# Decoder layer on one core: the first pair of the output projection in seven block products, with its weight sums and its loads in other places

## The chip, the cores and the metric

The kernel runs on one core of a Trainium2 chip. The metric is the device time of one execution in microseconds (us); the time of a kernel is the median of its runs. The engines are named PE (TensorE), DVE (VectorE), ACT (ScalarE), POOL (GpSimd) and SP (SyncE, which here only issues DMAs). Everything is float32.

## What is computed

One decoder layer over 2048 tokens (32 sequences of 64) of width 512: an attention with 32 heads of 128, a cross attention and a mixture of expert biases, each added to x. Only the attention's end matters here: every head's output is put beside the others to 4096 numbers per token, and the output projection `out @ Wo + bo` brings them back to 512.

```python
x = x + _L0_attn_ref(_layernorm(x), Wq, bq, Wk, bk, Wv, bv, Wo, bo, gq, gk)
#   ... per head: q, k, v; rmsnorm of q and k; softmax(q k^T * scale) @ v  -> out
#   return out @ Wo + bo          # (2048 x 4096) @ (4096 x 512)
x = x + _L0_xattn_ref(_layernorm(x), ctx_1024, ...)
x = x + _L0_ffn_ref(_layernorm(x), router_weight, router_bias, expert_bias)
```

## The kernel before

The 2048 tokens are 16 tiles of 128 rows. Two tiles (`t` = 2 pair, 2 pair + 1) are a pair, so there are 8 pairs; four tiles are a quad. The heads go in 16 groups of two. The main loop (L1259) runs over two halves of the tokens, and in each half over the 16 groups; a `Window` (L624) makes q, k and v of one group for the two quads of a half. The attention of a unit (one group, one quad; named 14_3 for group 14, quad 3) follows one window later, by a `Line` (L1153): `scale` multiplies k on POOL (L542) and q on DVE (L544) by the inverse roots `rs` that SP has fetched (L533), `attend` makes the scores on PE (L555), the softmax on DVE, ACT and POOL (L257 to L265), `turn` transposes the probabilities on PE (`pt_p`, L249), and the next `attend` mixes the values (L592), which ACT copies to `ot` (L607) and SP stores to HBM as `mixed` (L614).

When the last window is done, two units more have to be attended, 15_2 and 15_3, and 14_3 has to be finished. `drain` (L1358) does this, and fills PE's time between its steps with the output projection of pair 0. For that, three things are fetched: the mixtures of pair 0 (`a` with tile and head of the group: a0_0, a0_1, a1_0, a1_1; 1 MB each, L821), the weights Wo in four blocks B11, B12, B21, B22 of (head of the group, half of the columns), each in two parts of 1 MB (L809; `wo_0` holds B11 and B21, `wo010` and `wo011` are B12, `wo110` and `wo111` are B22), and the tiles x0, x1 of x.

Pair 0 is done plainly (`plain_out`, L850): for each of two tiles and two halves of the columns, two terms of 16 matmuls (`chunks`, L832, which yields every four matmuls, so that `drain` can count them), and an addition to x. Pairs 1 to 7 are done in Strassen-Winograd's form by `strassen_out` (L884): seven products of 16 matmuls instead of eight, numbered 1 to 7, with sums of mixtures (S) on the left and sums of weights (T) on the right. The weight sums are made once, by `wo_sums` (L864): two subtractions into `t1` and `t2` (L873, L874), one into `t4` (L878) for each half of the part index on DVE, and B22 - B12 (L881) on POOL. Each is an operation on 128 x 2048 numbers.

Pair 1's first products come next, and between them the small setup of the cross attention: `xw` and other weights are loaded, transposed (`pt_xw`, L1429), copied by ACT (`turned`), multiplied to `wqk`. From there `strassen_out` of pairs 1 to 7 yields every four matmuls, and `advance` (L1348) puts one step of the finished tiles' cross attention and experts (`after_attention`, L1105) in between.

What sets the order: PE, DVE, ACT and POOL follow the program's order up to `ordered.close()`; SP's queue is ordered by a scheduler, and so are DVE, ACT and POOL after that point. SP issues in order, and a DMA that has to wait for its buffer holds back those behind it. Buffers come from pools: `blocks` has seven of 1 MB, which hold the tokens' inputs of a half (x1 to x7) and later mixtures, weights and `t4`, and two of 4 MB, which hold the weights of the heads and later `wo_0` and `wo_t`; `xpool` has four of 256 KB for tiles of x and the bias (`bo_0`), so that x3 takes the place of `bo_0` when L825 has added the bias to x1.

The order in `drain` before, with `go(n)` for n steps of four matmuls:

```python
go(1); line.turn(); go(4); line.scale(); go(4); line.scale(); go(3); line.attend()
line.scale(); go(4); line.scale(); go(1); line.turn(); go(2); line.attend()
go(4); line.turn(); go(1); line.attend()
a12 = load_mixed(2, 1, block("a12_1"))
sums = wo_sums(wo_b)
next(sums)
for _ in fill: pass
```

Of the kernel before, what the change touches and what calls it, by code (L numbers as in the profile page):

```python
# [13 lines left out]
P = 128  # L14
# [27 lines left out]
def decoder_layer(  # L42
# [37 lines left out]
    def block(name):  # L80
        return blocks.tile([P, BLK], F32, tag="blk", name=name)
# [193 lines left out]
    class AttentionInput:  # L275
# [32 lines left out]
        def turn(self):  # L308
            pair = self.pair
            pt = [  # L310
                transposed(xt.rearrange("p (kc k) -> p kc k", k=P), f"a{2 * pair + i}", ps_s)
                for i, xt in enumerate(self.xs)
            ]
            half, t, j = pair // 4, pair // 2 % 2, pair % 2
            if pair % 4 == 0:


                halves_x[half] = {o: block(f"x{o}_{half}") for o in (1, 2, 4, 5, 6, 7, 3)}
            raw = {
                o: it[:, 0 : 8 * P].rearrange("p (c t j n) -> p c t j n", c=2, t=2, j=2)  # L320
                for o, it in halves_x[half].items()
            }
# [501 lines left out]
    def add_bias(xt):  # L824
        nc.gpsimd.tensor_tensor(xt, xt, bo_b, ALU.add)  # L825
# [21 lines left out]
    def out_block(name):  # L847
        return ps_a.tile([P, DH], F32, tag="pa", name=f"py_{name}")

    def plain_out(pair, a, b, done):  # L850
        ts = (2 * pair, 2 * pair + 1)
        xs = [load_x(t) for t in ts]
        for i, t in enumerate(ts):
            for n in range(2):
                py = out_block(f"{t}_{n}")
                yield from chunks(py, [(a[i][k], b[k][n]) for k in range(2)])
                to = xs[i][:, bass.ts(n, DH)]
                nc.vector.tensor_tensor(to, to, py, ALU.add)
                yield
        for t, xt in zip(ts, xs):  # L860
            add_bias(xt)
            done(t, xt)

    def wo_sums(b):  # L864

        four = four_blocks("wo_t")
        t1, t2 = (
            [it.rearrange("p (g f) -> p g f", f=DH) for it in two] for two in (four[0:2], four[2:4])
        )
        t4 = []  # L870
        for half in range(2):
            b11, b12, b21, b22 = (b[k][n][half] for k in range(2) for n in range(2))
            nc.vector.tensor_tensor(t1[half], b12, b11, ALU.subtract)  # L873
            nc.vector.tensor_tensor(t2[half], b22, t1[half], ALU.subtract)  # L874
            if half == 1:
                yield
            t4.append(block(f"wo_t4{half}").rearrange("p (g f) -> p g f", f=DH))
            nc.vector.tensor_tensor(t4[half], b21, t2[half], ALU.subtract)  # L878
        for half in range(2):
            b12, b22 = (b[k][1][half] for k in range(2))  # L880
            nc.gpsimd.tensor_tensor(b12, b22, b12, ALU.subtract)  # L881
        yield {1: b[0][0], 2: b[1][0], 3: b[1][1], 4: t4, 5: t1, 6: t2, 7: b[0][1]}

    def strassen_out(pair, right, done, a12=None):  # L884

# [373 lines left out]
    for n, (hg, half) in enumerate(groups):  # L1259
        w = weights.pop(n)  # L1260
        units = [HeadGroup(hg, 2 * half + t, w) for t in range(2)]
        prepare(n)
        if hg == 0:
            single(
                units[0],
                {
                    3: lambda: coming[0].norm(),
                    6: lambda: (coming.pop(0).turn(), coming[0].norm()),
                    11: lambda: coming.pop(0).turn(),
                },  # L1270
            )
# [25 lines left out]
        else:  # L1297
            more = {
                (0, 3): [lambda n=n: sums_of_next(n), lambda: make(1)],
                (1, 0): [lambda: make(1)],  # L1300
                (1, 3): [lambda: make(1)],
                (2, 3): [lambda: make(2)],
            }

            def also(n, m, it):
                more.setdefault((n, m), []).append(it)

            if hg == 1:
                for at, o in (
                    ((0, 0), 2),  # L1310
                    ((0, 1), 6),
                    ((0, 2), 3),
                    ((1, 0), 7),
                    ((1, 1), 3),
                    ((1, 2), 4),
                    ((2, 1), 4),
                ):
                    also(*at, lambda o=o: inner(o))
            if half == 0 and 2 <= hg < 2 + NT // 2:
                norm = normed_tile(NT // 2 + hg - 2)  # L1320
# [12 lines left out]
            if n + 1 == len(groups):  # L1333
                four = four_blocks("wo_0")
                wo_b = [[load_wo(k, 0, four[2 * k : 2 * k + 2])] for k in range(2)]
                a_0 = [[load_mixed(0, h, block(f"a0_{h}")) for h in range(HG)]]
            double(Window(units, w, half), more)
    for k in range(2):
        wo_b[k].append(load_wo(k, 1, [block(f"wo{k}1{i}") for i in range(2)]))


# [6 lines left out]
    def advance():  # L1348
        for it in list(tails):
            it[0] -= 1  # L1350
            if it[0] < 0:
# [3 lines left out]
                else:  # L1355
                    it[0] = wait

    def drain():  # L1358
        fill = iter(todo)

        def go(count):
            for _ in range(count):
                next(fill)
                take_waiting()

        go(1)
        line.turn()
        go(4)
        line.scale()
        go(4)  # L1370
        line.scale()
# [11 lines left out]
        go(1)  # L1383
        line.attend()
        a12 = load_mixed(2, 1, block("a12_1"))
        sums = wo_sums(wo_b)
        next(sums)
        for _ in fill:
            pass
        return a12, sums  # L1390

    rest = work.tile([P, BLK], F32, tag="qk", name="a1_1", bufs=4)
    bo_b = xpool.tile([P, D], F32, tag="x", name="bo_0")
    load(bo_b, bo.partition_broadcast(P))
    a_0.append([load_mixed(1, 0, block("a1_0")), load_mixed(1, 1, rest)])
    todo = plain_out(0, a_0, wo_b, start_tail)
    a12, sums = drain()
    assert not waiting and not coming
    ordered.close()
    phase.close()  # L1400
    work = ctx.enter_context(tc.tile_pool(name="output", bufs=2, reuse_waits="tile"))
    bo_b = work.tile([P, D], F32, tag="bo", name="bo_b", bufs=1)
    load(bo_b, bo.partition_broadcast(P))
    (right,) = sums
    outs = {1: strassen_out(1, right, start_tail, a12)}
    next(outs[1])

# [13 lines left out]
    nc.gpsimd.memset(eb_sb[NEXP:P, :], 0.0)  # L1421
    nc.gpsimd.memset(wds, 0.0)
    load(eb_sb[0:NEXP, :], eb)
    for _ in range(4):
        next(outs[1])

    pt = ps_t.tile([P, 2, P], F32, tag="pt", name="pt_xw")
    for j in range(2):
# [63 lines left out]
```

## Time and profile before

| | us |
|---|---|
| median of 3 runs | 1933.31 (1930.85 to 1934.56) |
| the profiled execution | 1932.7, its span 1930.9 |
| PE busy | 1887.6 (98%) |
| DVE, POOL, ACT busy | 1228.4, 1044.3, 646.8 |
| output projection on PE (L837): its two larger groups of matmul records | 262.5 (1152 records) and 144.3 (608 records) |

| stretch, us from the start | PE busy | DVE busy | granted PE clock | DMA share |
|---|---|---|---|---|
| 1350 to 1380, end of the last window | 29.78 of 30 | 20.26 | 1.00 | 0.95 |
| 1380 to 1400, pair 0 begins | 18.66 of 20 | 4.11 | 1.00 | 0.87 |
| 1400 to 1420 | 20.00 of 20 | 4.67 | 1.00 | 0.25 |
| 1420 to 1440 | 20.00 of 20 | 13.18 | 1.00 | 0.44 |
| 1440 to 1460, pair 1 begins | 14.57 of 20 | 15.06 | 0.94 | 0.31 |
| 1460 to 1480 | 18.29 of 20 | 6.46 | 0.89 | 0.39 |
| 1480 to 1500 | 20.00 of 20 | 10.22 | 0.91 | 0.19 |

In the lines of the timelines below, the columns are: start and length in us, engine, line, operation, output <- input by their names, shapes, and how many were merged; in brackets the idle time ahead of it and what ended it. A float32 matmul of PE leaves two records. Buffer numbers are left out of names, so `py` is any block of the projection, `wo_t` any of the weight sums.

### The profile page before, as it was taken

How to read it: one execution, taken by the hardware profiler on the slowest of the kernel's cores; microseconds unless marked ns; L12 is line 12 of the kernel's file. 1: busy time of each engine (PE TensorE's matmuls, PEld its weight loads, DVE VectorE, ACT ScalarE, POOL GpSimd, SP SyncE). 2: the span in 40 equal slices, each digit the busy share in tenths (PEclk: the TensorE clock that was granted, in tenths of full speed). 3: DMA queues.
4: the chain of work that ended last, by engine and by line, in shares of the span. 5: the costliest groups of instructions: out<-in, count | busy, mean ns of one | idle time of the engine just before them, and what ended most of it. 6: DMA issues, size and time to landing. Idle time of an engine off the chain costs nothing.

```text
span 1930.9 us, 40526 instructions
## 1 busy us (share of the span) xinstructions
PE 1887.6 (98%) x16877; PEld 1622.2 (84%) x16877; DVE 1228.4 (64%) x2024; ACT 646.8 (33%) x1579; POOL 1044.3 (54%) x812
## 2 busy tenths in 40 slices
PE   9999999999999999999999999999998999999997
PEld 8888888888888888888888888888886888888874
DVE  7867777676667659666666666666454545554554
ACT  2343344344333443344333434433311202221122
POOL 5856666665667539665666666565234323332320
PEclk9999999999999999999999999999998999999998
DMA  4244334334433343334433333444932231223100
GB/s 138 67 134 142 121 126 129 110 105 131 133 111 110 107 140 107 99 101 131 133 110 111 110 100 100 130 134 137 301 127 86 90 111 67 71 88 112 49 20 23
DMA packets 164568, 214.92 MB, mean 111 GB/s; under 512 B 10144, under 2 KB 135136, under 8 KB 160288
## 3 DMA queue, kind: packets, MB, share of 16 engines
q1 hardware_dynamic: 163200, 211.24, 34.1%
q8 instruction: 133, 2.18, 0.5%
q10 hardware_dynamic: 1184, 1.08, 0.2%
q14 instruction: 51, 0.42, 0.1%
HBM read 171.92 MB, written 40.37 MB: 110 GB/s over the span
## 4 chain that ended last, share of the span: by engine, by line
PE 76%; DVE 12%; POOL 7%; issue 3%; DMA 1%; ACT 1%; SPq 0%; POOLq 0%; DVEq 0%; ACTq 0%
PE p_w L655 24%; PE py L837 19%; PE va L387 7%; PE vb L387 6%; POOL qk L734 5%; PE ms_w L779 3%; PE s L555 3%; PE o L592 3%; DVE qk L666 3%; DVE qk L679 3%; DVE qk L544 1%; PE pt_p L249 1%; PE pa L445 1%; DVE sums L262 1%; PE py_x L1050 1%
## 5 line engine op out<-in xcount | busy, mean ns | idle before, releaser
L655 PE MATMUL p_w<-x,w 128*128 128x256 f32 x2940 | 723.9, 383 | 8.6 <-DVE qk L666 8.0
L655 PEld LDWEIGHTS p_w<-x,w 128*128 128x128 f32 x2940 | 521.2, 190 | 70.7 <-DVE qk L666 13.1
L666 DVE TENSOR_TENSOR qk<-p_w,qk 128x512 f32<-128x512 f32 x360 | 213.0, 600 | 135.0 <-PE p_w L655 99.1
L356 ACT ACTIVATE sq<-qk 128x512 f32<-128x512 f32 x256 | 158.1, 629 | 400.2 <-POOL qk L734 225.4
L387 PEld LDWEIGHTS va<-w,x 128*128 128x128 f32 x2048 | 263.6, 191 | 30.5 <-ACT v L403 20.6
L387 PE MATMUL va<-w,x 128*128 128x128 f32 x2048 | 276.1, 278 | 2.1 <-ACT v L403 2.1
L837 PE MATMUL py<-wo,a 128*128 128x256 f32 x1152 | 262.5, 381 | 0.0
L679 DVE TENSOR_TENSOR qk<-p_w,qk 128x512 f32<-128x512 f32 x360 | 220.1, 620 | 57.4 <-PE p_w L655 53.9
L120 POOL TENSOR_TENSOR w<-w 128x768 f32<-128x768 f32 x126 | 244.5, 1951 | 2.4
L837 PEld LDWEIGHTS py<-wo,a 128*128 128x128 f32 x1152 | 213.9, 190 | 35.6 <-issue 7.3
L265 POOL TENSOR_TENSOR prob<-prob,inv 128x512 f32<-128x512 f32 x64 | 75.3, 1177 | 294.9 <-DVE inv L264 291.7
L542 POOL TENSOR_TENSOR qk<-qk,rs 128x512 f32<-128x512 f32 x128 | 172.4, 1347 | 113.1 <-DMA rs<-row_w 92.9
L387 PEld LDWEIGHTS vb<-w,x 128*128 128x128 f32 x1536 | 201.4, 192 | 9.7
L387 PE MATMUL vb<-w,x 128*128 128x128 f32 x1536 | 202.4, 275 | 0.0
L403 ACT COPY v<-va 128x256 f32<-128x256 f32 x256 | 94.8, 370 | 308.9 <-PE va L387 308.7
L544 DVE SCALAR_TENSOR_TENSOR qk<-qk,gqk,rs 128x512 f32<-128x512 f32 x128 | 173.4, 1355 | 11.1 <-DMA rs<-row_w 10.0
L837 PE MATMUL py<-wo_t,a 128*128 128x256 f32 x608 | 144.3, 389 | 0.0
L837 PEld LDWEIGHTS py<-wo_t,a 128*128 128x128 f32 x608 | 116.1, 195 | 16.9 <-issue 0.8
L734 POOL TENSOR_TENSOR qk<-qk 128x512 f32<-128x512 f32 x60 | 90.7, 1511 | 61.1 <-DVE qk L679 58.7
L257 DVE TENSOR_REDUCE mx<-s 128x8 f32<-128x512 f32 x64 | 44.1, 689 | 106.8 <-PE s L555 106.8
L407 DVE TENSOR_TENSOR v<-vb,v 128x256 f32<-128x256 f32 x192 | 80.8, 421 | 45.6 <-PE vb L387 27.0
L607 ACT ACTIVATE ot<-o,bvt 128x256 f32<-128x256 f32 x256 | 99.2, 469 | 2.2 <-PE o L592 2.2
(182 smaller groups left out, 2198.2 us busy)
## 6 DMA issues: line engine op xcount, KB each, us to landing
rs<-row_w SPq DMA_DIRECT2D x120, 512.0 KB
mixed<-ot SPq DMA_DIRECT2D x64, 512.0 KB
a<-mixed SPq DMA_DIRECT2D x32, 1024.0 KB
w<-in_wq_dram SPq DMA_DIRECT2D x64, 256.0 KB
w<-in_wk_dram SPq DMA_DIRECT2D x62, 256.0 KB
w<-in_wv_dram SPq DMA_DIRECT2D x62, 256.0 KB
wo<-in_wo_dram SPq DMA_DIRECT2D x8, 1024.0 KB
x<-in_x_dram SPq DMA_DIRECT2D x20, 256.0 KB
```

The costliest lines, as they stand in the source:

```text
L120: on.tensor_tensor(*(it.rearrange("p c j d -> p (c j) d") for it in (out, a, b)), ALU.subtract)
L356: nc.scalar.activation(sq, of, AF.Square)
L387: nc.tensor.matmul(to[:, j, :], left[i][:, c, j, :], right[i][:, c, 2, :], start=first and j == 0 and c == 0, stop=c == 1, skip_group_chec ...
L403: nc.scalar.copy(self.v[h, ab], what)
L542: nc.gpsimd.tensor_tensor(k, k, rk, ALU.mult)
L544: lambda: nc.vector.scalar_tensor_tensor(q, q, gqk, rq, ALU.mult, ALU.mult)
L607: nc.scalar.activation(ot[:, h, :, b * SEQ : (b + 1) * SEQ], o[b][:, h, :, :], AF.Identity, bias=bvt[:, hg * HG + h : hg * HG + h + 1],)
L655: nc.tensor.matmul(bank[:, s, :], self.w.inner[o][i], inner_x[self.half, o][i], start=first and s == 0, stop=True, skip_group_check=True,)
L666: nc.vector.tensor_tensor(to(t, j), bank, add(t, j), ALU.add)
L679: nc.vector.tensor_tensor(to(t, j), bank, to(t, j), ALU.add)
L734: on.tensor_tensor(qk[to], qk[to], qk[what], ALU.add)
L837: nc.tensor.matmul(py, a[:, g, :], b[g // KH][:, g % KH, :], start=n == 0 and g == 0, stop=n == last and g == NHG - 1,)
```

## The change

- Pair 0 is done by `first_out`, in seven products in the order 1, 2, 3, 7, 5, 6, 4; the four sums of mixtures are made by DVE after the third to the sixth step of `drain`.
- The weight sums are made by DVE alone, one operation after each step from the ninth on.
- The mixtures of pair 0 are fetched inside the last window (a1_1 into a buffer of q and k, three into the `blocks`), ahead of the last weight blocks; B22 is fetched ahead of B12. The sum `s1` takes another buffer of q and k, `S4` a quarter of `wo_t`.
- `p1`, the first product, takes a buffer of `xpool`.
- The first `turn` in `drain` comes after two steps instead of one.
- Pair 1 goes six steps instead of four ahead of the setup of the cross attention, with `advance` called in the last two.
- The order in which the seven blocks x1 to x7 are asked for is another.

```diff
-                halves_x[half] = {o: block(f"x{o}_{half}") for o in (1, 2, 4, 5, 6, 7, 3)}
+                halves_x[half] = {o: block(f"x{o}_{half}") for o in (1, 2, 6, 5, 7, 3, 4)}
...
-    def plain_out(pair, a, b, done):
...
-    def wo_sums(b):
...
+    def wo_sums(b, places):
...
+        (b11, b12), (b21, b22) = b
+
+        def subtract(to, a, what):
+            nc.vector.tensor_tensor(to, a, what, ALU.subtract)
+
+        def make():
+            for half in range(2):
+                subtract(t1[half], b12[half], b11[half])
+                yield
+                subtract(b12[half], b22[half], b12[half])
+                yield
+            for half in range(2):
+                subtract(t2[half], b22[half], t1[half])
+                yield
+            for half in range(2):
+                t4.append(block(f"wo_t4{half}").rearrange("p (g f) -> p g f", f=DH))
+                subtract(t4[half], b21[half], t2[half])
+                yield
+
+        return {1: b11, 2: b21, 3: b22, 4: t4, 5: t1, 6: t2, 7: b12}, make()
+
+    def first_out(a, right, s4, s1, done):
+        (a11, a12), (a21, a22) = a
+        xa, xb = load_x(0), load_x(1)
+        la, ra, lb, rb_ = (xt[:, bass.ts(n, DH)] for xt in (xa, xb) for n in range(2))
+        p1 = xpool.tile([P, D], F32, tag="x", name="p1_0")[:, 0:DH]
+        def combine(op, to, x, y):
+            return lambda: nc.vector.tensor_tensor(to, x, y, op)
+
+        sums[3] = combine(ALU.add, s1, a21, a22)
+        sums[4] = combine(ALU.subtract, a21, a11, a21)
+        sums[5] = combine(ALU.subtract, a11, s1, a11)
+        sums[6] = combine(ALU.subtract, s4, a12, a11)
...
+        py = yield from product(1, a11)
+        nc.scalar.copy(p1, py)
+        nc.gpsimd.tensor_tensor(la, la, p1, ALU.add)
+        yield
+        py = yield from product(2, a12)
+        add(la, py)
+        yield
+        py = yield from product(3, s4)
+        add(ra, py)
+        yield
+        py = yield from product(7, a21)
+        add(lb, py)
+        add(rb_, py)
+        yield
+        py = yield from product(5, s1)
+        add(ra, py)
+        add(rb_, py)
+        yield
+        py = yield from product(6, a11)
+        add(p1, py)
+        for to in (ra, lb, rb_):
+            nc.gpsimd.tensor_tensor(to, to, p1, ALU.add)
+        add_bias(xa)
+        done(0, xa)
+        yield
+        py = yield from product(4, a22)
+        add(lb, py)
+        add_bias(xb)
+        done(1, xb)
...
-                a_0 = [[load_mixed(0, h, block(f"a0_{h}")) for h in range(HG)]]
...
+                also(2, 0, lambda: mixture(0, 1, lambda: block("a0_1")))
+                also(2, 1, lambda: mixture(1, 0, lambda: block("a1_0")))
+                also(2, 2, lambda: mixture(0, 0, lambda: block("a0_0")))
+                also(2, 2, lambda: mixture(1, 1, lambda: qk_buffer("a1_1")))
...
-    for k in range(2):
+    for k in (1, 0):
         wo_b[k].append(load_wo(k, 1, [block(f"wo{k}1{i}") for i in range(2)]))
...
             for _ in range(count):
-                next(fill)
+                next(todo, None)
+                done += 1
                 take_waiting()
-
-        go(1)
+                if done in sums:
+                    sums[done]()
+                elif done >= 9:
+                    next(making_wo, None)
+
+        go(2)
         line.turn()
-        go(4)
+        go(3)
         line.scale()
...
         line.attend()
         a12 = load_mixed(2, 1, block("a12_1"))
-        sums = wo_sums(wo_b)
-        next(sums)
-        for _ in fill:
-            pass
-        return a12, sums
...
+        go(4)
+        return a12
...
-    for _ in range(4):
+    for n in range(6):
         next(outs[1])
+        if n > 3:
+            advance()
```

More of the change, by code (lines that the diff above doesn't have):

```diff
@@ L848, in out_block @@
         return ps_a.tile([P, DH], F32, tag="pa", name=f"py_{name}")
-    def plain_out(pair, a, b, done):
[L851 to L862, printed above, removed]
@@ L864, in wo_sums @@
-    def wo_sums(b):
-        four = four_blocks("wo_t")
+    def wo_sums(b, places):
         t1, t2 = (
-            [it.rearrange("p (g f) -> p g f", f=DH) for it in two] for two in (four[0:2], four[2:4])
+            [it.rearrange("p (g f) -> p g f", f=DH) for it in two]
+            for two in (places[0:2], places[2:4])
         )
         t4 = []
[L871 to L875, printed above, removed]
-                yield
[L877 to L882, printed above, removed]
+        (b11, b12), (b21, b22) = b
[4 more added lines that the diff above has]
+                subtract(t1[half], b12[half], b11[half])
+                yield
+                subtract(b12[half], b22[half], b12[half])
[8 more added lines that the diff above has]
+        return {1: b11, 2: b21, 3: b22, 4: t4, 5: t1, 6: t2, 7: b12}, make()
@@ new lines, in first_out, with product, add @@
+    def first_out(a, right, s4, s1, done):
[9 more added lines that the diff above has]
+        sums[6] = combine(ALU.subtract, s4, a12, a11)
+        def product(i, it):
+            py = out_block(f"{i}_0")
+            yield from chunks(py, [(it, right[i])])
+            return py
+        def add(to, py):
+            nc.vector.tensor_tensor(to, to, py, ALU.add)
+        py = yield from product(1, a11)
[27 more added lines that the diff above has]
+        done(1, xb)
@@ L1335, in decoder_layer, with mixture, qk_buffer @@
                 wo_b = [[load_wo(k, 0, four[2 * k : 2 * k + 2])] for k in range(2)]
-                a_0 = [[load_mixed(0, h, block(f"a0_{h}")) for h in range(HG)]]
+                a_0 = [[None, None], [None, None]]
+                def mixture(t, h, place):
+                    a_0[t][h] = load_mixed(t, h, place())
+                def qk_buffer(name):
+                    return work.tile([P, BLK], F32, tag="qk", name=name, bufs=4)
+                also(2, 0, lambda: mixture(0, 1, lambda: block("a0_1")))
+                also(2, 1, lambda: mixture(1, 0, lambda: block("a1_0")))
+                also(2, 2, lambda: mixture(0, 0, lambda: block("a0_0")))
+                also(2, 2, lambda: mixture(1, 1, lambda: qk_buffer("a1_1")))
             double(Window(units, w, half), more)
-    for k in range(2):
+    for k in (1, 0):
         wo_b[k].append(load_wo(k, 1, [block(f"wo{k}1{i}") for i in range(2)]))
@@ L1356, in advance @@
                     it[0] = wait
+    sums = {}
+    bo_b = xpool.tile([P, D], F32, tag="x", name="bo_0")
+    load(bo_b, bo.partition_broadcast(P))
+    wo_t = four_blocks("wo_t")
+    s1 = qk_buffer("s1_0").rearrange("p (g n) -> p g n", n=P)
+    s4 = wo_t[3].rearrange("p (g n) -> p g n", n=P)
+    right, making_wo = wo_sums(wo_b, wo_t)
+    todo = first_out(a_0, right, s4, s1, start_tail)
     def drain():
-        fill = iter(todo)
+        done = 0
         def go(count):
+            nonlocal done
             for _ in range(count):
-                next(fill)
+                next(todo, None)
+                done += 1
                 take_waiting()
-        go(1)
+                if done in sums:
[3 more added lines that the diff above has]
+        go(2)
         line.turn()
-        go(4)
+        go(3)
         line.scale()
@@ L1385, in drain @@
         a12 = load_mixed(2, 1, block("a12_1"))
-        sums = wo_sums(wo_b)
-        next(sums)
-        for _ in fill:
-            pass
-        return a12, sums
[L1392 to L1397, printed above, removed]
+        go(4)
+        return a12
+    a12 = drain()
     assert not waiting and not coming
@@ L1403, in decoder_layer @@
     load(bo_b, bo.partition_broadcast(P))
-    (right,) = sums
     outs = {1: strassen_out(1, right, start_tail, a12)}
```

## The prediction, made before the changed kernel had run

> **What bounds the kernel now.** I read the page first (PE is busy 98% of the span; 76% of the chain that ended last is PE, and its second line is L837, the output projection), then PE's timeline over the end of the heads and the first two pairs, then VectorE's, POOL's and SP's there, then stretches of 1 us for the granted clock. All clock times are us from the span's start in the execution before.
>
> ```profile
> 1379.84 1.99 PE L837 MATMUL py<-wo,a 128*128 128x256 f32 x8
> 1383.17 0.66 PE L249 MATMUL pt_p<-ident,prob 128*128 128x128 f32 x4 [1.34 <-POOL prob L265]
> 1383.67 19.16 PE L837 MATMUL py<-wo,a 128*128 128x256 f32 x88
> ...
> 1417.65 1.15 PE L555 MATMUL s<-qk 128*64 128x64 f32 x32
> ...
> 1430.19 20.99 PE L837 MATMUL py<-wo,a 128*128 128x256 f32 x96
> 1451.01 1.89 PE L837 MATMUL py<-wo_t,a 128*128 128x256 f32 x8
> 1456.89 0.30 PE L1429 MATMUL pt_xw<-ident,xw 128*128 128x128 f32 x1 [3.99 <-POOL x L825]
> 1458.16 0.45 PE L1429 MATMUL pt_xw<-ident,xw 128*128 128x128 f32 x1 [0.97 <-DMA xw<-in_xwk_t_dram]
> ...
> 1459.66 7.68 PE L837 MATMUL py<-wo_t,a 128*128 128x256 f32 x24
> ```
>
> Each matmul leaves two records, so x88 is 44 matmuls; a record costs 19.1/88 = 0.217 us. PE has one large hole, 3.99 + 0.97 us at 1453 to 1458, and the 24 records behind it take 7.68 us where 24 x 0.217 = 5.2 are normal: the clock was at half.
>
> ```profile
> 1478.00:1479.00 1.00, 0.16 (x1) 0.00 (x0) 0.77 (x2) 1.00 (x8) 0.00 (x0) 1.00 0.00 0
> 1479.00:1480.00 1.00, 0.12 (x2) 0.13 (x4) 1.00 (x2) 1.00 (x6) 0.00 (x0) 1.00 0.00 0
> ...
> 1482.00:1483.00 1.00, 1.00 (x4) 0.82 (x3) 1.00 (x1) 0.00 (x0) 0.00 (x0) 0.50 0.00 0
> ```
>
> The columns are the busy us of PE, PEld, DVE, ACT and POOL, then the granted clock, DMA share and GB/s. The clock falls to 0.50 behind a hole of only 1.71 us as well. What makes the large hole is VectorE:
>
> ```profile
> 1429.54 2.28 DVE L873 TENSOR_TENSOR wo_t<-wo,wo 128x2048 f32<-128x2048 f32 x1
> 1431.86 2.29 DVE L874 TENSOR_TENSOR wo_t<-wo,wo_t 128x2048 f32<-128x2048 f32 x1
> 1434.19 6.48 DVE L878 TENSOR_TENSOR wo_t<-wo,wo_t 128x2048 f32<-128x2048 f32 x1
> ```
> ```profile
> 1433.99 4.53 POOL L881 TENSOR_TENSOR wo<-wo,wo 128x2048 f32<-128x2048 f32 x1 [7.34 <-PE py L837]
> 1443.02 6.56 POOL L881 TENSOR_TENSOR wo<-wo,wo 128x2048 f32<-128x2048 f32 x1 [4.49 <-DVE wo_t L873]
> ```
>
> A sum of two SBUF blocks takes 2.28 us on VectorE and 4.53 on POOL, and whichever starts second waits for the whole of the other (6.48 = 4.3 + 2.2). So the sums end at 1451.7; only then comes x1's addition (L858), POOL's L825 on x1, SP's load of x3 into the buffer that L825 frees, and behind it in SP's queue the xw loads that PE awaits.
>
> **The change, part by part.**
>
> *Fewer products.* 8 blocks of 16 matmuls become 7: 16 matmuls, 32 records x 0.217 = -6.9 us.
>
> *The hole goes.* With the sums made earlier, x1's last addition follows product 4 directly. From L858's end (1452.05) to the second pt_xw (1458.16) took 6.1 us; now PE has 28 matmuls (16 of pair 1's product 2, 12 of its product 4: 12.1 us) ahead of pt_xw, so 6 us of cover are left over. Gone: 3.99 + 0.97 + 2.4 (slow clock) = -7.4. Without the cover it would cost all of this again.
>
> *What comes instead: a queue on VectorE.* The built order of the changed kernel puts on VectorE, between the softmax of 14_3 and the scores of 15_3, four sums of mixtures, eight of weights, and the old work. I walk it with the rows' durations. The first sum starts as `inv` ends (1381.85); POOL's L265 comes 0.2 us later and waits for it, as here behind a 0.70 us operation, where it took 1.35 and not the 1.04 of 1382.08 (VectorE's row, then POOL's):
>
> ```profile
> 1362.12 0.70 DVE L544 SCALAR_TENSOR_TENSOR qk<-qk,gqk,rs 128x512 f32<-128x512 f32 x1
> ```
> ```profile
> 1362.38 1.35 POOL L265 TENSOR_TENSOR prob<-prob,inv 128x512 f32<-128x512 f32 x1 [3.52 <-DVE inv L264]
> ```
>
> So L265 ends at 1381.85 + 2.28 + 0.9 = 1385.05. PE has 8 matmuls instead of 4 before the transposition that awaits it and arrives at 1383.3: a hole of 1.7 instead of 1.34, +0.15 us net. The second sum runs to 1387.2; the third overwrites a0_0, so it waits for product 1 (1388.95) and ends at 1391.35; L544 0.7; the fourth (S4) ends at 1394.3, ahead of product 3, which begins at 1395.9: no cost, 1.6 us to spare. (If S4 is late, product 3 waits as long.) Then VectorE adds product 2 to x0 (1396.0 to 1396.4), and from there to the last scaling (L544) of 15_3 its queue holds:
> - 8 sums of weights x 2.28 = 18.2 (the two of L881 among them)
> - 3 x L544 at 0.62 from start to start (1362.12 to 1362.74) = 1.9; three additions of products 1.2; softmax of 15_2, start of mx to end of inv, 3.0 (in the row of 14_3: 1378.87 to 1381.9)
> - POOL's holds: rest of one L542 0.6, three L542 x 1.27, one L265 0.95 = 5.4
>
> Together 29.7: it ends at 1396.4 + 29.7 = 1426.1. PE without waits reaches the scores of 15_3 at 1417.65 + 0.15 = 1417.8; it loses 1.0 on the way (product 7's second half needs a sum ending at 1409.5, PE is there at 1408.5), 0.95 at the transposition of 15_2 (L265 behind a sum), and the rest, 6.3, at the scores: +8.25. Bounds: if POOL's holds fell wholly into VectorE's idle time, 5.4 less; if each POOL operation cost its own length once more, 5.4 more. I take the middle, as both rows above show one wait per meeting.
>
> *The clock behind that hole.* 6.3 us of idle PE against the 4.0 us that cost 2.4 and the 1.71 that cost 7.13 - 5.37 = 1.8 (24 records at 1480.97): +2.4, bounds 0 and 3.4.
>
> *Loads.* Bytes and number are unchanged. The mixtures take the places in SP's queue that three weight blocks had, behind the same releases, on DMA engines that are full from 1364 to 1382 in both; a0_0, issued at 1366.8, has 4.9 MB ahead of and with it at some 0.37 MB per us, lands near 1374 and is used at 1379.84. The last weight block (wo011) moves behind the rs loads, to 1385, lands near 1394 and is used at 1404.6. a12_1 (now in a0_0's place) is issued only after product 6, near 1437, 8 us before its use; a 1 MB load at 1402.86 took about 5. Behind it in SP's queue wait x2 (for POOL's three additions of p1, 2.2 us), the last `ot` store, bo_b, a22, a11, a21, x3, xw: about 1 us later relative to PE than before, against 6 us of cover. 0 us; without cover, 1. The new order of the x blocks moves nothing: every load still waits for the same releases. Copy L902 and POOL's additions lie behind products: 0.
>
> *After kv_0* PE's order is unchanged, and PE is full (100 of 100 us from 1600 to 1700, and from 1700 to 1800), so what is saved stays; the 1.71 us hole at 1478 stays too (0, bounds +-1.8, as the clock may or may not fall there).
>
> Sum: -6.9 - 7.4 + 0.15 + 8.25 + 2.4 = -3.5. The profiled execution took 1932.7 (span 1930.9); **1929.2**. It lies 0.6 below the median of 1933.31, within the runs' spread of 3.7, so nothing is shifted.
>
> [...]
>
> **Rivals.**
> - *VectorE keeps up* (0.26). POOL's holds mostly fall into waits, the scores of 15_3 wait 1 to 3 us and the clock stays: 1929.2 - 5.4 - 2.4 = 1921.4, up to 1926; with no stall at all 1932.7 - 14.3 = 1918.4. For: rs0 and rs1 of 15_3 may land later, under the softmax. Against: 18.2 us of sums alone stand against 21 us of PE work there.
> - *The clock falls at short holes too* (0.11), at 1383 and again at 1408 to 1415: + 1.8 to 3.6, 1931 to 1933. For: the row at 1478. Against: the hole of 1.34 us at 1382 left the clock at 1.00.
> - *The sums on VectorE take as long as on POOL* (0.04), each meeting with POOL costing more than one wait: 4.5 more, 1933.7. For: L878 took 6.48. Against: 2.2 of that is its own.
> - *Slower: POOL's queue behind x0* (0.13). The new addition of p1 to x0 (it needs x0 and ScalarE's copy) stands on POOL ahead of both L542 of 15_2, and VectorE's next addition waits for it. x0's load stands behind 1 MB of weights; I have it land at 1395. Each us later shifts VectorE's queue, the scores of 15_2 and the next rs loads by one: 3.5 us (1398.5) take the gain, 8.0 (1403) make the kernel 0.2% slower; 1938 for 8.8. For: DMA is full from 1384 to 1397. Against: before, another 1 MB block stood ahead of x0.
>
> **Chances.** 0.2% (3.9 us) is about what a measurement of this kernel can tell from no change: the bounds are 1929.4 and 1937.2. Forecast 0.46, own range 1926.5 to 1932, 0.28 of it below 1929.4. Faster 0.28 + 0.26 = 0.54; same 0.18 + 0.11 + 0.04 = 0.33; slower 0.13. The range 1921 to 1935.5 leaves out the slower rival and about 0.06 of the first.
>
> **What would show it.** Product blocks: 112 matmuls (224 records) for pair 0. A wait of PE of about 6 us at the scores (L555) of 15_3 put down to DVE's L544; L265 of 14_3 at about 3 us; no wait of PE at pt_xw beyond the copy of `turned`; a stretch at clock 0.50 behind the scores. Wrong: no hole at L555 (then VectorE keeps up), holes at product 3 (S4 late), or L903-type additions on POOL starting after 1400.

## The result, and the profile after

| | before | changed |
|---|---|---|
| median, us | 1933.31 (5 runs, 1930.85 to 1934.56) | 1925.16 (5 runs, 1923.74 to 1927.31) |
| ratio to before, 95% interval | | 0.9966 [0.9955, 0.9977] |
| profiled execution; its span | 1932.7; 1930.9 | 1925.16; 1923.3 |
| PE busy; records of PE | 1887.6; 16877 | 1878.1; 16845 |
| DVE busy | 1228.4 | 1232.1 |

The kernel became faster by 8.1 us in the medians, 6.6 by the ratio, 7.6 in the two spans. 1929.2 was predicted, 1921 to 1935.5 as its range, with 0.54 for faster. The gain came, and the time lies inside the range; the way there differs in three places.

Three marks cut each profiled execution into four stretches: the start of the scores of 14_3 (PE's L555 with 32 records at about 1379), the start of the first `pt_x` (PE's L249 at about 1485), and the start of the large wait of PE (3.71 us, ahead of `pt_f`) near the end:

| us | before | changed |
|---|---|---|
| start to the scores of 14_3 | 1377.67 | 1379.34 |
| the stage: from there to the first `pt_x` | 110.27 | 103.17 |
| from `pt_x` to the large wait near the end | 415.68 | 415.69 |
| from there to the end | 27.28 | 25.10 |

The third row shows that nothing is gained or lost behind the stage. The first and the last row differ by no more than they do among the runs below that leave these parts alone (see the end), so **-7.10 us in the stage** is what the change did. Stages are compared below; each is from one profiled execution, and block_order shows that two of nearly the same work can differ by 0.4 us.

PE's timeline of the changed kernel in that stage (start, us, engine, line, operation, out and in, sizes, records, then in brackets the wait ahead of it and what ended it):

```profile
1386.69 0.66 PE L249 MATMUL pt_p<-ident,prob 128*128 128x128 f32 x4 [1.46 <-POOL prob L265]
1387.19 10.53 PE L837 MATMUL py<-wo,a 128*128 128x256 f32 x48
1397.55 7.07 PE L837 MATMUL py<-wo,wo_t 128*128 128x256 f32 x32
...
1410.88 3.72 PE L837 MATMUL py<-wo,a 128*128 128x256 f32 x16 [0.44 <-DVE wo L860]
...
1416.95 0.66 PE L249 MATMUL pt_p<-ident,prob 128*128 128x128 f32 x4 [0.62 <-POOL prob L265]
...
1420.99 0.45 PE L555 MATMUL s<-qk 128*64 128x64 f32 x8
1426.59 1.55 PE L555 MATMUL s<-qk 128*64 128x64 f32 x24 [5.15 <-DVE qk L544]
1428.07 1.99 PE L592 MATMUL o<-probt,v 64*64 64x64 f32 x64
1429.98 2.16 PE L837 MATMUL py<-wo_t,s 128*128 128x256 f32 x8
...
1460.13 0.62 PE L1496 MATMUL pt_xw<-ident,xw 128*128 128x128 f32 x2 [0.36 <-DMA xw<-in_xwq_t_dram]
...
1465.15 0.46 PE L1050 MATMUL kv<-ct,wqk 128*128 128x128 f32 x2 [1.73 <-DMA ct<-in_ctx_dram]
...
1476.14 1.16 PE L1060 MATMUL e_x<-kvs,xn_x 64*128 64x128 f32 x16
```

Product 3 (1397.55) follows without a wait: S4 was in time. The scores of 15_3 can do their first 8 records and then wait 5.15 us for VectorE. At `pt_xw` the hole of 3.99 + 0.97 us is gone, but a new wait of 1.73 us stands at `kv`, and the second `e_x`, which had a wait of 1.71 us before, has none. VectorE in front of that 5.15 us wait:

```profile
1417.37 5.55 DVE L860 TENSOR_TENSOR wo_t<-wo,wo_t 128x2048 f32<-128x2048 f32 x2
1422.84 0.74 DVE L899 TENSOR_TENSOR x<-x,py 128x256 f32<-128x256 f32 x2
1423.51 2.28 DVE L860 TENSOR_TENSOR wo_t<-wo,wo_t 128x2048 f32<-128x2048 f32 x1
1425.71 0.74 DVE L544 SCALAR_TENSOR_TENSOR qk<-qk,gqk,rs 128x512 f32<-128x512 f32 x1
```

The scaling L544 is the last in a row of sums that it does not need. The granted clock there (columns: PE, PEld, DVE, ACT, POOL busy us, clock, DMA share, GB/s):

```profile
1423.00:1424.00 1.00, 0.00 (x0) 0.00 (x0) 1.00 (x3) 0.00 (x0) 0.00 (x0) 0.76 0.00 0
...
1429.00:1430.00 1.00, 1.00 (x41) 0.88 (x35) 0.67 (x1) 0.30 (x1) 0.00 (x0) 0.50 0.00 0
1430.00:1431.00 1.00, 1.00 (x8) 0.92 (x5) 0.00 (x0) 1.00 (x4) 0.00 (x0) 0.82 0.07 16
```

It falls 2 us into the hole and comes back some 4 us after PE has resumed; 6.8 us in all.

### The profile page after: what moved, and what is told of

It reads as the page before. It is cut to its first block, busy times and chain, and to the rows that moved or that the text cites. A ratio compares the mean times of both kernels' runs of the same rounds, so it can differ in the third digit from the quotient of the medians.

```text
span 1923.3 us, 40481 instructions
## 1 busy us (share of the span) xinstructions
PE 1878.1 (98%) x16845; PEld 1615.8 (84%) x16845; DVE 1232.1 (64%) x2034; ACT 647.7 (34%) x1580; POOL 1042.6 (54%) x814
## 4 chain that ended last, share of the span: by engine, by line
PE 74%; DVE 12%; POOL 7%; issue 3%; DMA 2%; ACT 1%; SPq 0%; POOLq 0%; DVEq 0%; ACTq 0%
PE p_w L655 24%; PE py L837 17%; PE va L387 7%; PE vb L387 6%; POOL qk L734 5%; PE ms_w L779 3%; PE o L592 3%; PE s L555 3%; DVE qk L666 3%; DVE qk L679 3%; DVE qk L544 2%; PE pt_p L249 1%; DMA x<-in_x_dram 1%; PE pa L445 1%; DVE sums L262 1%
## 5 line engine op out<-in xcount | busy, mean ns | idle before, releaser
L265 POOL TENSOR_TENSOR prob<-prob,inv 128x512 f32<-128x512 f32 x64 | 78.7, 1230 | 298.2 <-DVE inv L264 295.0
L837 PE MATMUL py<-wo,a 128*128 128x256 f32 x992 | 227.5, 381 | 0.4 <-DVE wo L860 0.4
L837 PEld LDWEIGHTS py<-wo,a 128*128 128x128 f32 x992 | 183.7, 190 | 32.3 <-issue 7.3
L544 DVE SCALAR_TENSOR_TENSOR qk<-qk,gqk,rs 128x512 f32<-128x512 f32 x128 | 171.7, 1342 | 3.9 <-DMA rs<-row_w 2.3
L837 PE MATMUL py<-wo_t,a 128*128 128x256 f32 x672 | 154.7, 381 | 0.0
L837 PEld LDWEIGHTS py<-wo_t,a 128*128 128x128 f32 x672 | 125.2, 190 | 17.3 <-issue 0.8
L407 DVE TENSOR_TENSOR v<-vb,v 128x256 f32<-128x256 f32 x192 | 80.7, 420 | 45.7 <-PE vb L387 27.2
L257 DVE TENSOR_REDUCE mx<-s 128x8 f32<-128x512 f32 x64 | 44.1, 689 | 96.4 <-PE s L555 96.4
```

Source lines behind the costliest of these rows:

```text
L544: lambda: nc.vector.scalar_tensor_tensor(q, q, gqk, rq, ALU.mult, ALU.mult)
L837: nc.tensor.matmul(py, a[:, g, :], b[g // KH][:, g % KH, :], start=n == 0 and g == 0, stop=n == last and g == NHG - 1,)
```

## The experiments

All but the last start from the changed kernel. Ratios are to the kernel before, run beside them; the changed kernel has 0.9966 and a stage of 103.17 us.

| label | median, us (runs) | ratio, 95% | stage, us |
|---|---|---|---|
| t4_late | 1919.82 (5) | 0.9936 [0.9924, 0.9948] | 96.97 |
| twice | 1925.85 (6) | 0.9964 [0.9952, 0.9977] | 101.65 |
| eight_early | 1922.50 (6) | 0.9948 [0.9933, 0.9962] | 100.61 |
| sums_on_pool | 1927.39 (7) | 0.9967 [0.9955, 0.9979] | 103.10 |
| xw_first | 1924.72 (5) | 0.9963 [0.9951, 0.9975] | 103.36 |
| four_steps | 1930.65 (12) | 0.9995 [0.9986, 1.0003] | 109.03 |
| best1 | 1918.92 (6) | 0.9932 [0.9916, 0.9948] | 96.28 |
| block_order | 1924.48 (4) | 0.9960 [0.9945, 0.9974] | 102.79 |
| ct_early | 1927.50 (11) | 0.9980 [0.9971, 0.9989] | 103.43 |
| ct_early_neg | 1923.37 (5) | 0.9952 [0.9938, 0.9965] | 101.54 |
| best2 | 1914.65 (5) | 0.9908 [0.9894, 0.9922] | 92.54 |
| best2_twice | 1918.47 (6) | 0.9934 [0.9921, 0.9946] | 98.00 |

### t4_late: the last two sums behind the scores

```diff
-                elif done >= 9:
+                elif 9 <= done <= 14 or done >= 20:
                     next(making_wo, None)
```

> The changed kernel with one edit: VectorE makes the two sums of t4 (the last two of the eight sums of weights) after the scores of 15_3 instead of before them. Theory (VectorE's queue sets the scores of 15_3): the 5.15 us wait at L555 shrinks to under 0.6, the stretch at clock 0.50 behind it (1.8 us) goes, and product 4 has its t4 in time: 1925.2 - 4.9 - 1.8 = 1918.5. Rival (the rs1 load or POOL's scaling of 15_3 is late by itself): the wait stays near 5 and the time at 1925. Second rival (the late sums hold up the softmax of 15_3 or product 4): the wait moves to the transposition of 15_3 or to product 4, 1922 to 1925.

1919.82 (expected 1918.5), stage 6.20 us shorter. PE's rows with a wait at product 7, the scores of 15_3 and the second `e_x`:

```profile
1411.20 3.72 PE L837 MATMUL py<-wo,a 128*128 128x256 f32 x16 [1.18 <-DVE wo L860]
...
1422.51 0.92 PE L555 MATMUL s<-qk 128*64 128x64 f32 x24 [0.75 <-DVE qk L544]
...
1469.50 1.16 PE L1060 MATMUL e_x<-kvs,xn_x 64*128 64x128 f32 x16 [0.72 <-ACT kvs L1054]
```

5.15 became 0.75 (expected under 0.6) and the 24 records take 0.92 instead of 1.55 us: the granted clock stayed at 1.00. The rs1 load was not late, and neither the softmax nor product 4 waits for the late sums. A wait at `e_x` appears, to which the later runs come back.

### twice: 16 matmuls more in front of the scores

```diff
             py = out_block(f"{i}_0")
+            if i == 7:
+                for g in range(NHG):
+                    nc.tensor.matmul(
+                        py,
+                        it[:, g, :],
+                        right[i][g // KH][:, g % KH, :],
+                        start=g == 0,
+                        stop=g == NHG - 1,
+                    )
             yield from chunks(py, [(it, right[i])])
```

> The changed kernel with product 7 computed twice (16 matmuls more, 32 records, 6.9 us of PE work, ahead of the scores of 15_3; its first result is overwritten). Theory (PE waits for VectorE there anyway): the extra work fills the waits at the transposition of 15_2 (0.62) and at the scores (5.15) and spares the slow clock (1.8): 1925.2 + 6.9 - 7.6 = 1924.5, no change. Rival (time goes with PE's work; the wait at the scores moves along with PE): 1932.

1925.85 against 1925.16 (ratios 0.9964 and 0.9966), the stage even 1.52 us shorter: 6.9 us of work cost nothing, the rival's 1932 is out. PE has no wait at the transposition of 15_2 nor at the scores; its row there is x32 in one piece.

### eight_early: the sums early, but eight products

```diff
-            for half in range(2):
-                subtract(t1[half], b12[half], b11[half])
-                yield
-                subtract(b12[half], b22[half], b12[half])
-                yield
+            for half in range(2):
+                subtract(t1[half], b12[half], b11[half])
+                yield
...
+            for half in range(2):
+                subtract(b12[half], b22[half], b12[half])
+                yield
...
-    todo = first_out(a_0, right, s4, s1, start_tail)
+    todo = plain_out(0, a_0, wo_b, start_tail)
...
-                elif done >= 9:
+                elif 9 <= done <= 12 or done in (20, 21, 29, 30):
...
-        go(4)
+        go(9)
         return a12
```

`plain_out` is the kernel before's; the last two weight blocks are loaded in its order, too.

> Only the second half of the change: the first pair again in 8 plain block products (128 matmuls), but with the sums of weights made by VectorE beside it (t1 and t2 ahead of the scores of 15_3, t4 behind them, the differences in place of b12 last), no sums of mixtures, and the loads and the rest as in the changed kernel. Theory (the gain over the kernel before is the hole at pt_xw and its slow clock; the 16 matmuls saved by seven products are given back at VectorE's queue): against the changed kernel + 6.9 for the matmuls, - 7.7 for its four waits in the drain (1.46, 0.44, 0.62, 5.15), - 1.8 for the clock: 1922.6, and the waits in the drain under 1 us together. Rival (the seven products bring the gain): 1925.2 + 6.9 = 1932.

1922.50 us (expected 1922.6). Its timeline of PE at the scores of 15_3 and at the second `e_x`:

```profile
1418.01 1.15 PE L555 MATMUL s<-qk 128*64 128x64 f32 x32
...
1472.13 1.16 PE L1075 MATMUL e_x<-kvs,xn_x 64*128 64x128 f32 x16 [1.71 <-ACT kvs L1069]
```

With 16 matmuls more than the changed kernel it is not slower: in the changed kernel, what the seven products saved was given back at VectorE's queue. The other parts of the change, with the weight sums out of PE's way, are worth the whole gain over the kernel before without the seven products (ratio 0.9948). This run also makes the sums of t4 behind the scores, as t4_late does. Beside t4_late, its stage is 3.64 us longer, 1.7 of it by the slow clock behind `e_x`: with t4 late, the seven products are worth some 2 of their 6.9 us.

### sums_on_pool: two of the sums back on POOL

```diff
-                subtract(b12[half], b22[half], b12[half])
+                nc.gpsimd.tensor_tensor(b12[half], b22[half], b12[half], ALU.subtract)
```

> The changed kernel with the two differences of weights in place of b12 made by POOL instead of VectorE (as the kernel before had them). Theory (a POOL operation on two SBUF blocks shuts VectorE's sums out for its whole 4.53 us): VectorE's queue does not shrink by 2 x 2.28 but grows by 2 x (4.53 - 2.28) = 4.5, product 7 and the scores of 15_3 wait longer, 1925.2 + 4.5 = 1929.7. Rival (the engines share the work): the queue is 4.6 shorter, the wait at the scores falls under 1 us, 1918.8.

Neither: ratio 0.9967, stage 103.10. POOL's rows, then VectorE's:

```profile
1398.64 4.97 POOL L866 TENSOR_TENSOR wo<-wo,wo 128x2048 f32<-128x2048 f32 x1
1405.83 4.51 POOL L866 TENSOR_TENSOR wo<-wo,wo 128x2048 f32<-128x2048 f32 x1 [2.23 <-DVE wo_t L860]
```
```profile
1399.15 6.61 DVE L860 TENSOR_TENSOR wo_t<-wo,wo 128x2048 f32<-128x2048 f32 x1
...
1406.01 0.68 DVE L257 TENSOR_REDUCE mx<-s 128x8 f32<-128x512 f32 x1
```

The first POOL sum shuts VectorE out for its whole length, as told (6.61 = 4.4 of waiting + 2.2). The second runs beside the softmax of 15_2, whose reductions (L257, L262) have one input and keep their 0.68 us; some 3.2 us of its 4.51 are free. So the price was 4.5 - 3.2 = 1.3, and VectorE's queue from the start of `inv` of 14_3 to the last L544 grew by 1.1, from 43.1 to 44.2. PE's waits moved (0.42 and 3.02 at product 7, 2.46 at the scores); their sum hardly changed (5.90 instead of 6.21). PE came to the scores 1.1 us later and made up 1.0 of it before `kv`, 0.36 of that at `pt_xw`, where it no longer waits.

### xw_first: the small loads ahead of two mixtures

```diff
             a22 = load_mixed(tb, 1, beside("a12"))
+            between()
         a11 = load_mixed(ta, 0, beside("a11"))
...
```

`between` does the memset and the eight loads of xw, which stood behind `next(outs[1])`.

> The changed kernel with one edit: the eight small loads of xw stand in SP's queue behind the first mixture of pair 1 (a22) instead of behind all three and x3. Theory (xw and ct land late only because SP's queue stands still behind the 1 MB mixtures, 2.98 us at xwv and more at xws): the waits of PE at pt_xw (0.36) and at kv_0 (1.73) go, 1925.2 - 2.1 = 1923.1. Rival (the mixtures, now issued later, become the wait): a hole at product 4 or 1 of pair 1, 1925 to 1928.

Neither reason held: 1924.72, stage +0.19, which is no difference. The wait at `pt_xw` went, the one at `kv` fell from 1.73 to 1.39, and 1.18 us appeared at the second `e_x` (why, is shown at ct_early).

### four_steps: the last edit undone

```diff
-    for n in range(6):
+    for _ in range(4):
         next(outs[1])
-        if n > 3:
-            advance()
```

> The changed kernel with its last edit undone: four steps of pair 1 instead of six ahead of pt_xw, and the tail of x0 not advanced between them. Theory (these 8 matmuls are the cover of the xw loads, which land at a fixed time): PE is at pt_xw 3.5 us earlier and waits 0.36 + 3.5 = 3.9 us there, the clock falls behind it (2.0), and the wait for ct at kv_0 (1.73) goes: 1925.2 + 3.5 + 2.0 - 1.7 = 1929.0. Rival (the cover is worth nothing, since what is not done before pt_xw is done behind it and the clock stays): 1925 or a little under.

1930.65 (expected 1929.0); the stage is 5.86 us longer. PE's rows:

```profile
1459.81 0.71 PE L1494 MATMUL pt_xw<-ident,xw 128*128 128x128 f32 x2 [2.92 <-DMA xw<-in_xwq_t_dram]
...
1480.86 1.16 PE L1060 MATMUL e_x<-kvs,xn_x 64*128 64x128 f32 x16 [1.71 <-ACT kvs L1054]
```

The cover is needed: without it PE waits 2.92 us at `pt_xw` (expected 3.9). The wait for `ct` at `kv` goes, as expected, but 1.71 us come back at `e_x`; behind both the clock falls to 0.50.

### best1: four edits together

The steps of the sums (below), the sums of mixtures in two halves each, x0 and x1 loaded ahead of the last two weight blocks, and the edit of xw_first.

```diff
-                elif done >= 9:
+                elif done in (9, 10, 11, 12, 17, 18, 20, 21):
...
-            return lambda: nc.vector.tensor_tensor(to, x, y, op)
+            def two():
+                for g in (slice(0, KH), slice(KH, NHG)):
+                    nc.vector.tensor_tensor(to[:, g, :], x[:, g, :], y[:, g, :], op)
+
+            return two
...
```

> The changed kernel with four edits that the runs so far point to: t2 made after the last scaling of 15_3, t4 after its scores; each sum of mixtures in two halves, so that POOL's L265 waits for half a sum; x0 and x1 loaded ahead of the last weight blocks, so that POOL's addition of p1 does not hold VectorE for 1.8 us; the xw loads as in the run before last. Theory (VectorE's queue and SP's queue make all that is left of PE's waits here): of the waits 1.46, 0.44, 0.62, 5.15, 0.36 and 1.73 about 0.5 stay, and the slow clock (1.8) goes: 1925.2 - 9.3 - 1.8 = 1914.1; a wait of 0.7 to 1.7 for kvs at the second e_x, as with t4 late, may come back: up to 1916. Rival (the waits reappear at the loads, as PE then runs 10 us ahead of them): 1919 or more, with waits named DMA.

1918.92, close to the rival's 1919 and far from 1914.1. In the drain the waits are down to 0.40 and 0.27, but further on:

```profile
1455.76 0.46 PE L1055 MATMUL kv<-ct,wqk 128*128 128x128 f32 x2 [2.96 <-DMA ct<-in_ctx_dram]
1456.06 0.39 PE L1056 MATMUL kv<-xw,ct 128*128 128x128 f32 x2
1456.28 5.30 PE L837 MATMUL py<-wo,a 128*128 128x256 f32 x16
```

PE came earlier than `ct`, whose load stands behind two mixtures, and 16 records then took 5.30 us, where 3.62 is normal: the granted clock was 0.50 for 3.4 us from 1456.44.

### block_order: a part that should do nothing

```diff
-for o in (1, 2, 6, 5, 7, 3, 4)}
+for o in (1, 2, 4, 5, 6, 7, 3)}
```

> The changed kernel with the order of the x blocks as in the kernel before. Theory (every load waits for the same releases in either order): no difference, 1925.2 within 1.5. Rival (the mixtures find their places later and the first sum of mixtures or product 3 waits): 1927 or more.

1924.48, no difference, as expected. Two things in its profile show what chance can do. The stage is 0.38 us shorter with nothing in the edit that should shorten it. And 362 us behind the first `pt_x`, PE waits 1.92 us for `kvs`, as it does for 1.92 or 1.93 us in all kernels here that keep `neg_x` on VectorE (see below): only in this execution was the clock at 0.50 behind it, and the stretch from `pt_x` to the large wait took 417.30 us instead of 415.68.

### ct_early and ct_early_neg: are the waits at `kv` and at `e_x` one?

```diff
             a22 = load_mixed(tb, 1, beside("a12"))
+            between(0, 1)
         a11 = load_mixed(ta, 0, beside("a11"))
+        if between:
+            between(2, 3)
...
```

`between(0, 1)` loads xw (q, k) and the first `ct`, `between(2, 3)` loads xw (v, s).

> The changed kernel with the loads of xw (q and k) and of the first ct right behind a22 in SP's queue, ahead of a11. Theory (the wait for ct at kv_0 and the wait for kvs at the second e_x are one wait in two places: both hang on POOL's second sum of pair 1, whose end does not move, so what PE does not wait at kv_0 it waits at e_x; their sum was 1.7 in the kernel before, 1.7 in the changed one, 1.5 with t4 late): the waits at pt_xw and kv_0 go and 1.7 us come back at e_x, with the slow clock behind them as in the kernel before (1.8): 1925.2 - 0.4 + 1.8 = 1926.6, at best 1924.8 where the clock stays. Rival (the wait for ct is lost time of its own): 1923.1 and no wait at e_x.

1927.50 (expected 1926.6). No wait is left at `pt_xw` and `kv`, and the stage is 0.26 us longer than in the changed kernel, which is no difference. The clock stays at 1.00 behind the wait at `e_x`, where it was expected to fall. PE, VectorE and POOL:

```profile
1461.13 1.89 PE L837 MATMUL py<-wo_t,a 128*128 128x256 f32 x8
1462.86 0.38 PE L1055 MATMUL kv<-ct,wqk 128*128 128x128 f32 x2
...
1476.66 1.16 PE L1065 MATMUL e_x<-kvs,xn_x 64*128 64x128 f32 x16 [2.82 <-ACT kvs L1059]
```
```profile
1470.41 3.01 DVE L1078 TENSOR_SCALAR neg_x<-mx_x 128x4 f32<-128x4 f32 x2
```
```profile
1468.80 4.52 POOL L1012 TENSOR_TENSOR a<-a,a 128x2048 f32<-128x2048 f32 x1
```

Two products of 128 x 4 numbers take 3.01 us and end at 1473.4, when POOL's sum ends (1473.3). ScalarE's exponentials wait for them, `kvs` stands behind these on ScalarE, and PE waits for `kvs`. The same holds in the kernel before (`neg_x` 3.06 us, until 1476.6; POOL's sum until 1476.5). POOL's two sums begin when PE ends the product ahead of `kv`; in the changed kernel, where that was at 1463.42:

```profile
1463.51 4.51 POOL L1008 TENSOR_TENSOR a<-a,a 128x2048 f32<-128x2048 f32 x1 [2.50 <-PE py L837]
1468.10 4.51 POOL L1009 TENSOR_TENSOR a<-a,a 128x2048 f32<-128x2048 f32 x1
```

From the end of that product to the second `e_x` it took 12.52 to 12.54 us in the kernel before, t4_late, twice, eight_early, sums_on_pool, four_steps and block_order, although the wait at `kv` ran from 0 to 1.01 us and the one at `e_x` from 0.46 to 1.71. So a wait of PE between that product and `e_x` gives POOL time to finish: the two waits are one. (In the changed kernel the 1.73 us at `kv` were a little more than POOL needed: 12.72.) Its size was 1.7 in the theory and is 2.82 here, because POOL now has x3's addition (1.27 us) between its two sums; so it has in xw_first, and both took 13.63 to 13.64.

The next run takes `neg_x` off VectorE:

```diff
-            nc.vector.tensor_scalar(neg, mx, -(SEQ**-0.5), None, ALU.mult)
+            nc.scalar.activation(neg, mx, AF.Copy, scale=-(SEQ**-0.5))
```

> The run before with one edit more: the 128 x 4 product that makes neg_x goes from VectorE to ScalarE. Theory (neg_x, with one SBUF input, waits on VectorE until POOL's sum of two SBUF blocks has ended, 3.06 us for two where 0.29 is its own; ScalarE has no such wait): neg_x is ready 2.8 us earlier, the wait at the second e_x goes, and with it the slow clock: 1926.6 - 3.5 = 1923.1. Rival (the exponentials on ScalarE ahead of kvs make that wait, not neg_x): 1926.6, and 1.7 at e_x.

1923.37 (expected 1923.1), and no wait at `e_x`; from the product to `e_x` it takes 10.74 us now. ScalarE's and PE's rows:

```profile
1470.36 0.20 ACT L1078 ACTIVATE neg_x<-mx_x 128x4 f32<-128x4 f32 x1 [6.06 <-DVE mx_x L1076]
1471.98 0.21 ACT L1078 ACTIVATE neg_x<-mx_x 128x4 f32<-128x4 f32 x1
1472.08 0.38 ACT L1059 COPY kvs<-kv 128x256 f32<-128x256 f32 x1
```
```profile
1474.19 1.16 PE L1065 MATMUL e_x<-kvs,xn_x 64*128 64x128 f32 x16
```

`kvs` also moved ahead of the second four exponentials in ScalarE's order, which counts 1.4 us; behind all eight it would be ready at about 1473.9, still in time, but this was not tried apart. The edit also removes the later wait of 1.92 us for `kvs`, 362 us behind `pt_x`: from there to the large wait near the end it is 413.88 us now, 1.80 less. That the time was met is partly luck: 1.8 us of the expected 3.5 were for a slow clock that ct_early did not have, and the 1.80 us behind the stage, which had not been expected, stand in their place.

### best2 and best2_twice: all of it, and its check

best2 is best1 with the edits of ct_early_neg in place of xw_first.

> All edits that the runs point to: the first combination, with the loads of xw and ct and neg_x on ScalarE as in the two runs before. Theory (its wait of 2.96 us for ct and the half clock behind it, 5.30 us for 16 matmul records where 3.46 are normal, go, and the wait at the second e_x does not come back): 1918.9 - 2.96 - 1.84 = 1914.1. Rival (the wait comes back at another load, as PE is ahead of the DMA queues here): 1917 to 1919, and a wait named DMA.

1914.65 us (expected 1914.1), ratio 0.9908: 17 us under the kernel before and some 11 under the changed one (0.0058 in the ratio). Of the expected 4.8 us under best1 the stage brings 3.74; another 1.80 come from the later wait, as in ct_early_neg. What PE still waits for in the drain, then the scores of 15_3:

```profile
1382.86 0.66 PE L249 MATMUL pt_p<-ident,prob 128*128 128x128 f32 x4 [0.40 <-POOL prob L265]
...
1394.66 7.17 PE L837 MATMUL py<-wo,wo_t 128*128 128x256 f32 x32 [0.78 <-DVE wo_t L888]
...
1408.02 3.72 PE L837 MATMUL py<-wo,a 128*128 128x256 f32 x16 [0.36 <-DVE wo L860]
...
1417.29 1.15 PE L555 MATMUL s<-qk 128*64 128x64 f32 x32
```

best2_twice adds the edit of twice.

> The second combination with product 7 computed twice, as in the run on the changed kernel, where the same 16 matmuls cost 0.7 us. Theory (a matmul costs its time only where PE does not wait for another engine behind it; in this kernel no wait over 0.8 is left ahead of the scores of 15_3): 1914.7 + 6.9 - 0.4 = 1921.2. Rival (there is still slack that extra work fills, or PE's work is not what sets this stage): 1915 to 1918.

1918.47; the stage grows by 5.46 us, the ratio by 0.0026 (5.0 us). The same 16 matmuls that cost nothing in the changed kernel cost most of their 6.9 us here, after they have filled the 0.78 and 0.36. The expected 1921.2 is within the runs (1917.06 to 1923.70), but their median lies nearer to the rival's 1918; the stage and the ratio speak for the theory. So fewer matmuls do pay once no other queue stands in front of PE.

## Why the prediction was right, and where not

The stage term by term, the prediction's sum against the rows of the changed kernel:

| term | predicted | measured |
|---|---|---|
| 16 matmuls fewer | -6.9 | -6.9 (32 records fewer) |
| hole at `pt_xw` and its slow clock | -7.4 | -7.0 (0.36 left) |
| transposition of 14_3 | +0.15 | +0.12 (1.46 for 1.34) |
| VectorE's queue | +8.25 | +6.21 (0.44 + 0.62 + 5.15) |
| clock behind it | +2.4 | +1.74 (0.67 at s, 0.81 at o, 0.26 at py) |
| second `e_x` (the hole at 1478) | 0 | -3.40 (its 1.71, and the slow clock behind it, 6.97 - 5.28) |
| `ct` at `kv` | 0 | +1.73 |
| sum | -3.5 | -7.5; the stage itself is 7.10 shorter |

The rows leave 0.4 us unexplained.

- **The main steps held.** The hole at `pt_xw` went with the order of the sums; four_steps shows that its cover is real. VectorE's queue took the place, at the line and on the tile that were named, and t4_late and twice show that the queue, not a load, sets it. L265 of 14_3 took 2.90 us (about 3 predicted), product 3 did not wait.
- **A size was off:** "it loses 1.0 on the way", at product 7's second half, "0.95 at the transposition of 15_2" and "the rest, 6.3, at the scores". Measured 0.44, 0.62 and 5.15. VectorE's queue took 28.2 us from the end of the addition to x0 to the end of L544 instead of 29.7; POOL's holds came to 4.7 instead of 5.4, by the lengths of the rows above 2.28 and 0.70; and the sums, counted at 2.28 us each, follow each other at 2.20 from start to start, 0.6 for the eight. A quarter of the scores (0.45 us) does not need the last scaling.
- **A step failed:** "the 1.71 us hole at 1478 stays too". I had taken it for a fixed price and not asked what ends it. It ends with POOL's second sum of pair 1, which lets `e_x` begin 12.5 us behind the product ahead of `kv`; a wait of PE between that product and `e_x` takes its place.
- **A step failed:** "Loads ... 0 us". The 6 us of cover were nearly enough for `xw` (0.36 left over), not for `ct`, which comes last in SP's queue. That cost 1.73, and by the step before it nearly paid for itself. The 1.69 us of slow clock behind the second `e_x` went as well, and that is luck: behind the 1.71 us there the clock fell to 0.50 in the kernel before, behind the 1.73 us at `kv` it stayed at 1.00 in the changed one (see the end).
- **Of the rivals,** VectorE keeping up named the time (1921.4 to 1926) but not the reason: the wait and the slow clock were there. The clock did not fall at the short holes of 1.46, 0.44 and 0.62. The sums did not take POOL's time on VectorE (2.28 each where POOL was idle, not 4.53), so the 4.5 of that rival, two sums at 2.25 more, did not come. x0's addition on POOL began at 1397.05, 1395.4 by the clock of the kernel before, as assumed, and held VectorE 1.81 us; the slower case did not come.

So the forecast's time was 4 us high: one wait was over-sized by 2.0, its clock by 0.7, and a third wait, taken as constant, was traded for another of its size, while its slow clock (1.7) went; the 0.36 left at `pt_xw` goes the other way. In the stage alone the forecast was 3.6 us high (7.10 against 3.5); the last 0.5 lies in the first and the last stretch, where the change did nothing.

## What to carry to other kernels

Before counting saved matmuls as saved time, ask which queue stands in front of PE behind them: here 16 matmuls more cost 0 us as long as sums stood ahead of the scaling that PE's scores need, and over 5 when they did not. Put work with a late due time behind the short operation on which the bottleneck waits; that one line (t4_late) brought 6.2 us in the stage, where the whole change had brought 7.1. And when a wait disappears and the time stays, look for the next operation that hangs on the same event, as with `ct` and `kvs`.

## What was not expected of the hardware

- **A 128 x 4 product waited for POOL.** `neg_x` on VectorE, with one input in SBUF, took 3.01 to 3.06 us for two where it began early beside POOL's sum of two SBUF blocks (the kernel before, eight_early, four_steps, ct_early), and 0.28 to 0.29 for two in the stage without it; `mx_x`, which reads PSUM, was not held (1.28 to 1.29 for two beside that sum, 1.27 to 1.28 without it). In all seven runs whose rows show `neg_x` on VectorE beside that sum, it ends 0.1 us behind it, whether that made it 1.09 us long (the changed kernel) or 3.06. I had assumed that only operations with two SBUF inputs are held. One SBUF input alone does not decide it, though: in sums_on_pool the reduction L262 (0.69) and the reciprocal L264 (0.20) read SBUF beside POOL's second sum and were not held; in the softmax of 14_3, with no sum on POOL, they took the same 0.69 and 0.20. What sets them apart from `neg_x`, no run here shows.
- **When the clock fell was not a matter of the hole's length alone.** Holes up to 1.47 us never lowered it in this stage. One of 1.71 at the second `e_x` did, to 0.50, in all three kernels that had it (before, eight_early, four_steps); one of 1.73 at `kv` and one of 2.82 (ct_early) did not; 2.46, 2.92, 2.96, 3.02, 3.99 and 5.15 did.
- **The falls of one execution lay whole multiples of 3.41 us apart.** The stretches at 0.50 in the stage lasted 3.41 or 6.83 us. In the kernel before two begin at 1457.56 and 1481.45, seven times 3.41 apart; in four_steps three at 1424.30, 1461.84 and 1482.32, eleven and six times; in the changed kernel the one of the stage at 1423.53 and the next at 1901.39, 140 times. With the time cut every 3.41 us from the falls on, the three holes of 1.71 us lie wholly in the piece ahead of their fall (in the kernel before PE was idle for 50% of it); the 1.73 us at `kv` are parted into 1.06 and 0.67, the 2.82 us of ct_early into 1.26 and 1.56, and there the clock stayed at 1.00. In the kernel before and the changed one PE was idle for 50 to 98% of the piece ahead of each of their ten falls, by the profile's busy time. That is not all: in the kernel before it was idle for 55.5% of the piece from 1846.68, which holds the later wait of 1.92 us for `kvs`, the clock stayed at 1.00, and why stays open. So holes of nearly the same size cost 1.7 us of slow clock or nothing here.
- **The runs' spread sits in two places.** From the start to the scores of 14_3 the profiled executions took 1375.8 to 1379.9 us; from the large wait near the end to the end 25.0 to 25.3 or 27.2 to 28.2: in the shorter group the first stretch at 0.50 lasts 3.4 us, in the longer one 6.8 us or more. In between, from `pt_x` to that wait, ten of them agree within 0.02 us (415.67 to 415.69); block_order is 1.6 longer, the three with `neg_x` on ScalarE 1.8 shorter.
